# Layer 0 of a four-layer graph network: products of the matrices in two runs of four instead of in turn

## The chip, the cores and the metric

The kernel runs on one core of a Trainium2 chip as one program. The metric is the device time of one execution in microseconds. The engines are named as in the profile: PE is TensorE (PEld its weight loads), DVE is VectorE, ACT is ScalarE, POOL is GpSimd, and SP is SyncE, which here only issues DMAs.

## The reference

A graph has 8192 nodes with 32 features and 262144 edges, sorted by destination. Four layers follow each other, each of the form x = layernorm(x + layer(x)).

```
edge_index = jnp.stack([src, dst])
x = _layernorm(x + _L0_gnn_ref(x, L0_gnn_weight, src, dst, edge_type_64), axis=-1)   # sum over edges of x[src] @ weight[type]
x = _layernorm(x + _L1_gnn_ref(x, edge_index, edge_weight), axis=-1)                 # sum over edges of x[src] * edge_weight
x = _layernorm(x + _L2_gnn_ref(x, edge_index), axis=-1)                              # sum over edges of x[src]
x = _layernorm(x + _L3_gnn_ref(...), axis=-1)                                        # MLP on edge features, then messages and sums
```

In layer 0 each edge takes its source's features times one of 64 matrices of 32 x 32, and the results are summed by destination. Layers 1 and 2 sum plain features of the sources, with and without a weight per edge. In these two an edge's contribution depends only on (source, destination, weight), which do not change between layers.

## The kernel before

**Layer 0 itself.** A table `ytab` of x times every one of the 64 matrices is written to DRAM first. The edges are then taken in 256 groups of 8 tiles of 128 edges (`GG` = 256, `GT` = 8). For each group g, GpSimd gathers the rows of the table by 8 indirect DMAs (`gathers`, recorded at L454). VectorE builds one-hot matrices of the destinations (`pairs`, L583) and splits the gathered rows into three bfloat16 parts (`parts`, L858 to L863). TensorE multiplies the two, 8 matmuls (L897), which sums the rows by destination. VectorE collects a bank of sums every four groups (`bank_out`, L869). As soon as 1024 nodes have all their sums, `windows` (L575) puts them in place and `normalize` (L525 and the lines after it) adds and normalizes; the result goes to `x_b`.

**The matrices.** While layer 0 waits for its gathers, the same loop also builds two dense matrices for layers 1 and 2: for each destination node the weights and the counts of its edges by source, as a matrix of 128 x 64 each (source = low 7 bits by high 6 bits). `matrices(i)` does this for 32 destination nodes, 256 times in all, between groups 8 and 207. Each destination node has 64 slots for edges, and two nodes share the 128 partitions: the lower 64 hold one node's slots, the upper 64 the other's. VectorE makes one-hot matrices for 16 pairs of nodes: `oh_k` for the high bits (L638), `oh_l` for the low bits (L640), and `oh_k` times the weights (L643). There are two buffers of each (index b = i % 2), and VectorE waits for `oh_used[b]` before it writes one again.

TensorE then goes through four units (q = 0 to 3) of 8 products each (L654). A product has 64 slots as contraction, `oh_l` of one node (64 x 128) as weights and `oh_k` of the node (64 x 128: 64 columns of counts, 64 of weights) moving, all float32. It goes to one bank of PSUM: `two[:, h]` for h = 0 the lower node, h = 1 the upper node; j is the place of the product in the bank. A unit therefore fills two banks, and two units alternate (`pair_free[u]`). ScalarE evicts a unit by two instructions, the counts (L658) to 8 bits and the weights (L659) to float32. SyncE stores both to DRAM (`amat`, L664, 1 MB, and `cmat`, L666, 256 KB) once the four units are done.

**Layer 1 inside the loop.** Where a part of the matrices and of `x_b` is ready, layer 1 begins early: `layer1(g)` multiplies 1 MB pieces of `amat` that SyncE loads again (L695) with `x_b` (`products`, L717), 16 passes each. ScalarE takes a finished sum (L726), and in the next group TensorE turns it back (`turn_back`, L736) and VectorE adds it (`add_up`, L752). The list of which piece comes in which group is computed when the program is built (`plan`).

**The order of the work.** Every engine has one queue, in the order in which the program was written. For a group g that is:

```
pairs(oh[:, h], P, rel_b[:, g * GT:(g + 1) * GT])
PE.after(parts(g))
...                          # 8 matmuls at L897, marked as sums_of[g]
turn_back()
fetch_rows(g + AHEAD, 0, sums_of[g])
...                          # matrices(made): one or two for each group from 8 to 207
add_up()
fetch_rows(g + AHEAD, 1, now(PE))
layer1(g)
```

`AHEAD` is 12 here: GpSimd's first four gathers of group g + 12 wait for the sums of group g, and the last four for TensorE's last mark, which is the end of the matrices of group g. `Flow.after` is a wait on a semaphore, `Flow.mark` lets an instruction raise one.

After group 255, layers 1 and 2 are completed from the stored matrices, and layer 3 gathers, multiplies and sums again by edges. None of that is in the change.

Of the kernel before, what the change touches and what calls it, by code (L numbers as in the profile page):

```python
# [203 lines left out]
def raw_layers(tc, x, a, w0, w1, b1, w2, si, m, bad):  # L204
# [35 lines left out]
    def now(f):  # L240
        return (f.sem, f.n)

    def own(f, ins):

        mk = f.mark(ins)
        f.after(mk)
        return mk
# [383 lines left out]
    def matrices(i):  # L631

        b, pp, k0 = i % 2, i // 2, 16 * (i % 2)
        if i % WB == 0:
            V.after(now(V))
            own(V, V.e.tensor_copy(w_ps, meta_w.rearrange("p n k -> p (n k)")[:, i * 16:(i + WB) * 16]))
        V.after(oh_used[b])
        own(V, V.e.tensor_tensor(oh_k[:, b, :, 0, :], iota2[:, None, 0:64, 0].to_broadcast([P, 16, 64]),  # L638
                                 meta_k[:, pp, k0:k0 + 16, None].to_broadcast([P, 16, 64]), op=OP.is_equal))
        V.e.tensor_tensor(oh_l[:, b], iota2[:, None, :, 0].to_broadcast([P, 16, P]),  # L640
                          meta_l[:, pp, k0:k0 + 16, None].to_broadcast([P, 16, P]), op=OP.is_equal)
        wo = (i % WB) * 16
        vm = V.mark(V.e.tensor_tensor(oh_k[:, b, :, 1, :], oh_k[:, b, :, 0, :],  # L643
                                      w_ps[:, wo:wo + 16, None].to_broadcast([P, 16, 64]), op=OP.mult))
        PE.after(vm)
        for q in range(4):
            u = units[0] % 2
            units[0] += 1
            PE.after(pair_free[u])
            two = bank[:, 2 + 2 * u:4 + 2 * u, :]  # L650
            for j in range(4):
                for h in range(2):
                    hs_ = slice(64 * h, 64 * h + 64)
                    ins = PE.e.matmul(two[:, h].rearrange("p (c s j) -> p c s j", s=64, j=4)[:, :, :, j],  # L654
                                      oh_l[hs_, b, 4 * q + j, :], oh_k[hs_, b, 4 * q + j], start=True, stop=True)
            pm = PE.mark(ins)
            A.after(pm, st_ld[b].mark() if q == 0 and st_ld[b].n else None)
            A.e.activation(st_c[:, b, q], two[:, :, 0:256], AF.Copy)  # L658
            pair_free[u] = am = A.mark(A.e.activation(  # L659
                st_a[:, b, :, q].rearrange("p z h w -> p h z w"),  # L660
                two[:, :, 256:512].rearrange("p h (z w) -> p h z w", w=32), AF.Copy))
        oh_used[b] = pm
        S.after(am)
        st_ld[b].add(S.e.dma_start(amat[i // 128][i // 8 % 16, :, 0:P * 2048].rearrange("z (p w) -> p z w", w=2048)[:, :, 256 * (i % 8):256 * (i % 8 + 1)],  # L664
                                   st_a[:, b].rearrange("p z q h w -> p z (q h w)")))
        stored[i] = st_ld[b].add(S.e.dma_start(cmat[i], st_c[:, b].rearrange("p u h c -> p (u h c)")))  # L666
# [211 lines left out]
    for g in range(GG + 2):  # L878
# [9 lines left out]
        h, bk, c = g % NO, (g // per) % 2, g % per  # L888
# [13 lines left out]
        if g >= FIRST:  # L902
            upto = min(CB, (g - FIRST + 1) * CB // SP1)
            while made < upto:
                matrices(made)
                made += 1
# [835 lines left out]
```

## Time and profile before

| what | value |
|---|---|
| median of 10 runs | 5775.37 us (5768.69 to 5782.47) |
| profiled execution | 5773.13 us |
| its span, from first to last instruction | 5771.3 us |
| busy in the span: PE, DVE, POOL, ACT | 82%, 76%, 72%, 33% |
| weight loads (PEld) | 58% |
| mean granted TensorE clock | 0.893 |
| first and last instruction at L654 | about 362 and 2398 us |
| last gather of layer 0 issued, last normalization begun (L575) | 2805 us, 2811 us |

The page gives for each engine the time in which it did work. It also cuts the span into 40 slices of 144 us, with the busy share of each in tenths, and lists groups of instructions by line with their busy time, the mean duration of one, and the idle time of the engine before them with what ended it. [...] Row counts of matmuls and loads are passes: a float32 product takes two.

### The profile page before, as it was taken

To read this page: it belongs to the slowest core of one execution; us is meant where nothing else is said; L and a number is where in the kernel's file an instruction comes from. 1 tells how busy PE (TensorE), PEld (TensorE's weight loads), DVE (VectorE), ACT (ScalarE), POOL (GpSimd) and SP (SyncE) were. 2 spreads that over 40 slices of the span, in tenths; PEclk is the share of its full clock that TensorE was granted. 3 is DMA by queue.
4 is the path that set the end of the run, shared out by engine and by line. 5 is a ranking of instruction groups with operands and counts; after the bars stand their busy time and mean duration, and the time that the engine had idled before them with its cause. 6 is when DMAs were issued, how large, how long until landed. Compare 5 with 4: busy or idle time off the path is not lost.

```text
span 5771.3 us, 89081 instructions
## 1 busy us (share of the span) xinstructions
PE 4713.7 (82%) x34726; PEld 3355.1 (58%) x34726; DVE 4398.8 (76%) x9510; ACT 1894.0 (33%) x3067; POOL 4141.5 (72%) x4236
## 2 busy tenths in 40 slices
PE   7456677767777788644499999999999999999998
PEld 3146666666666666423255566666666666666665
DVE  4268898989989898543355788788787878888887
ACT  5255555555555555310176111111111111111110
POOL 2677777777777777777366777777777777777775
PEclk8578888989899899766699899999999999999999
DMA  9636666769789899955475111111111111111111
GB/s 344 223 100 201 190 211 223 253 229 330 243 299 315 281 339 324 350 176 203 187 279 197 26 26 30 30 26 30 26 30 30 26 30 26 30 26 30 30 26 22
DMA packets 583102, 865.29 MB, mean 150 GB/s; under 512 B 102605, under 2 KB 441614, under 8 KB 549134
## 3 DMA queue, kind: packets, MB, share of 16 engines
q1 hardware_dynamic: 448094, 782.68, 38.4%
q0 software_dynamic: 134144, 73.67, 6.6%
q8 instruction: 275, 4.51, 0.3%
q10 hardware_dynamic: 432, 3.15, 0.2%
q14 instruction: 157, 1.29, 0.1%
HBM read 454.28 MB, written 404.88 MB: 149 GB/s over the span
## 4 chain that ended last, share of the span: by engine, by line
PE 27%; POOL 10%; DMA 6%; DVE 4%; issue 4%; ACT 0%; POOLq 0%; DVEq 0%; ACTq 0%
PE bank L1203 11%; POOL f_arena L454 10%; PE bank L1194 9%; DMA f_arena<-fxtab,f_src 5%; PE bank L1033 4%; PE bank L1170 2%; DVE f_arena L1238 1%; PE bank L575 1%; DMA f_arena<-famat 1%; DVE f_arena L1234 1%; DVE f_arena L588 0%; PE bank L717 0%; PE bank L980 0%; DVE f_arena L1136 0%; DVE f_arena L1231 0%
## 5 line engine op out<-in xcount | busy, mean ns | idle before, releaser
L454 POOL DMA_INDIRECT f_arena<-fytab,f_row x2048 | 1957.2, 956 | 652.2 <-issue 548.6
L454 POOL DMA_INDIRECT f_arena<-fxtab,f_src x2048 | 1947.3, 951 | 643.1 <-issue 518.6
L654 PE MATMUL bank<-f_arena 64*128 64x128 f32 x16384 | 1195.8, 303 | 404.8 <-DVE f_arena L643 277.7
L654 PEld LDWEIGHTS bank<-f_arena 64*128 64x128 f32 x16384 | 1100.0, 210 | 484.8 <-DVE f_arena L643 302.6
L1203 PE MATMUL bank<-f_arena 128*128 128x344 f32 x4096 | 1311.2, 463 | 0.0
L1194 PE MATMUL bank<-f_arena 65*128 65x256 f32 x4096 | 1022.1, 393 | 79.0 <-DVE f_arena L1238 79.0
L1178 ACT ACTIVATE f_arena<-bank,f_arena 64x512 f32<-64x512 f32 x512 | 350.7, 685 | 2121.4 <-PE bank L1170 2114.8
L1194 PEld LDWEIGHTS bank<-f_arena 65*128 65x128 f32 x4096 | 771.1, 193 | 432.2 <-DVE f_arena L1238 145.7
L1203 PEld LDWEIGHTS bank<-f_arena 128*128 128x128 f32 x4096 | 799.2, 195 | 357.5 <-issue 29.8
L658 ACT ACTIVATE f_arena<-bank 128x512 uint8<-128x512 f32 x1024 | 613.1, 599 | 839.7 <-PE bank L654 742.5
L659 ACT ACTIVATE f_arena<-bank 128x512 f32<-128x512 f32 x1024 | 612.1, 598 | 0.0
L640 DVE TENSOR_TENSOR f_arena<-bank,f_arena 128x2048 f32<-128x2048 bf16 x256 | 586.6, 2292 | 8.7
L1238 DVE TENSOR_TENSOR f_arena<-bank,f_arena 128x256 f32<-128x256 f32 x1536 | 550.4, 413 | 0.0
L897 PE MATMUL bank<-f_arena 128*128 128x96 bf16 x2048 | 150.7, 225 | 313.0 <-DVE f_arena L863 312.9
L1134 DVE TENSOR_TENSOR f_arena<-f_arena 128x192 f32<-128x192 f32 x256 | 92.0, 359 | 408.0 <-DMA f_arena<-fxtab,f_src 406.4
L717 PE MATMUL bank<-f_arena,f_x_b 128*32 128x256 f32 x4096 | 307.9, 440 | 89.3 <-DMA f_arena<-famat 71.4
L588 DVE TENSOR_TENSOR f_arena<-bank,f_rel 128x512 f32<-128x512 f32 x512 | 348.7, 681 | 0.0
L1234 DVE TENSOR_TENSOR f_arena<-bank,f_arena 128x512 f32<-128x512 f32 x512 | 348.4, 680 | 0.0
L897 PEld LDWEIGHTS bank<-f_arena 128*128 128x128 bf16 x2048 | 109.6, 107 | 395.8 <-DVE f_arena L863 308.4
L638 DVE TENSOR_TENSOR f_arena<-bank,f_arena 128x1024 f32<-128x1024 bf16 x256 | 311.9, 1219 | 14.1 <-PE bank L654 12.0
L643 DVE TENSOR_TENSOR f_arena<-f_arena,bank 128x1024 f32<-128x1024 f32 x256 | 309.6, 1209 | 0.0
L802 POOL CAST f_arena<-f_arena 128x1536 bf16<-128x1536 uint8 x62 | 169.0, 2737 | 160.0 <-PE bank L717 70.3
(147 smaller groups left out, 4389.9 us busy)
## 6 DMA issues: line engine op xcount, KB each, us to landing
famat<-f_arena SPq DMA_DIRECT2D x256, 1024.0 KB
f_arena<-famat SPq DMA_DIRECT2D x256, 1024.0 KB, 12.0
fytab<-f_arena SPq DMA_DIRECT2D x64, 1024.0 KB, 11.9
fcmat<-f_arena SPq DMA_DIRECT2D x256, 256.0 KB
f_arena<-fcmat SPq DMA_DIRECT2D x16, 4096.0 KB, 14.4
f_arena<-fytab,f_row POOLq DMA_INDIRECT x2048
f_arena<-fxtab,f_src POOLq DMA_INDIRECT x2048
f_arena<-laid_ea SPq DMA_DIRECT2D x64, 512.0 KB, 3.4
```

Of the source, the lines that this page charges most:

```text
L454: return G.e.indirect_dma_start(out=dest, out_offset=None, in_=table, in_offset=bass.IndirectOffsetOnAxis(ap=ix, axis=0))
L588: return V.e.tensor_tensor(o, iota[:, None, :].to_broadcast([P, n, P]), rel[:, t:t + n, None].to_broadcast([P, n, P]), op=OP.is_equal)
L638: own(V, V.e.tensor_tensor(oh_k[:, b, :, 0, :], iota2[:, None, 0:64, 0].to_broadcast([P, 16, 64]), meta_k[:, pp, k0:k0 + 16, None].to_broa ...
L640: V.e.tensor_tensor(oh_l[:, b], iota2[:, None, :, 0].to_broadcast([P, 16, P]), meta_l[:, pp, k0:k0 + 16, None].to_broadcast([P, 16, P]), o ...
L654: ins = PE.e.matmul(two[:, h].rearrange("p (c s j) -> p c s j", s=64, j=4)[:, :, :, j], oh_l[hs_, b, 4 * q + j, :], oh_k[hs_, b, 4 * q + j ...
L658: A.e.activation(st_c[:, b, q], two[:, :, 0:256], AF.Copy)
L659: pair_free[u] = am = A.mark(A.e.activation(st_a[:, b, :, q].rearrange("p z h w -> p h z w"), two[:, :, 256:512].rearrange("p h (z w) -> p ...
L1178: quad[q + h] = dict(h=A.mark(A.e.activation(hs[0:64, (q + h) % 4], bank[64 * h:64 * h + 64, 2, :], AF.Relu, bias=b1_s[64 * h:64 * h + 64])))
L1194: ins = PE.e.matmul(wp[:, t, :], hs[0:65, q % 4, t * P:(t + 1) * P], w2_s[0:65], start=True, stop=True)
L1203: ins = PE.e.matmul(bank[:, g % 2, 0:MW], oh[:, c % NO, t, :], p[:, c % NP, t, :], start=(c % 2 == 0 and t == 0), stop=(c % 2 == 1 and t = ...
L1234: V.e.tensor_tensor(pq[:, :, 0:128].rearrange("p t (o k) -> p t o k", k=16), wp[:, :, 0:128].rearrange("p t (o k) -> p t o k", k=16), a0[: ...
L1238: ins = V.e.tensor_tensor(pq[:, :, 128 + 64 * mm:192 + 64 * mm].rearrange("p t (o i) -> p t o i", i=8), wp[:, :, 192:256].rearrange("p t ( ...
```

## The change

In each unit the two loops are exchanged. Before, the products go lower, upper, lower, upper (the j-th product of both nodes side by side). After, four products on the lower 64 partitions come first, then four on the upper 64. The operands, the places of the results, the number of instructions on every engine, and all waits and marks are the same; the unit's mark stands on the last product, which is the same product in both (j = 3, h = 1).

```diff
             two = bank[:, 2 + 2 * u:4 + 2 * u, :]
-            for j in range(4):
-                for h in range(2):
+            for h in range(2):
+                for j in range(4):
                     hs_ = slice(64 * h, 64 * h + 64)
                     ins = PE.e.matmul(two[:, h].rearrange("p (c s j) -> p c s j", s=64, j=4)[:, :, :, j],
                                       oh_l[hs_, b, 4 * q + j, :], oh_k[hs_, b, 4 * q + j], start=True, stop=True)
             pm = PE.mark(ins)
```

## The prediction

> **What bounds the kernel now.** I read the page's slices first, one slice being 144 us.
>
> ```profile
> PE   7456677767777788644499999999999999999998
> DVE  4268898989989898543355788788787878888887
> POOL 2677777777777777777366777777777777777775
> PEclk8578888989899899766699899999999999999999
> ```
>
> The change lives in layer 0, slices 3 to 19. TensorE is at 6 to 8 there, VectorE at 8 and 9, and GpSimd's 7 never moves. The groups of instructions explain GpSimd's flat 7, and show the matmuls of L654, the line that is reordered.
>
> ```profile
> L454 POOL DMA_INDIRECT f_arena<-fytab,f_row x2048 | 1957.2, 956 | 652.2 <-issue 548.6
> L654 PE MATMUL bank<-f_arena 64*128 64x128 f32 x16384 | 1195.8, 303 | 404.8 <-DVE f_arena L643 277.7
> ```
>
> A gather takes 0.944 us (median) and then 0.30 us before the next one is issued ("issue": it waits for nothing). In windows, the stretch that holds all of L654:
>
> ```profile
> core 0: us, PE busy (x) PEld busy (x) DVE busy (x) ACT busy (x) POOL busy (x), PEclk, DMA share, GB/s
> 360.00:2400.00 2040.00, 1536.13 (x21208) 1328.83 (x21208) 1823.25 (x2428) 1111.71 (x2167) 1542.03 (x1635) 0.90 0.79 265
> ```
>
> 1635 gathers in 2040 us are one per 1.248 us: GpSimd is never free. A group of edges needs 8 gathers, so the pace is 9.98 us a group. The chain of waits says the same at the end of layer 0: gather, issue, gather, issue, up to the last gather at 2805 us, and then 6 us to the first matmul of the last normalization. So GpSimd bounds layer 0. VectorE (1823 of 2040 us) is close behind; TensorE has 504 us idle: 278 us waiting for VectorE's L643, 121 for ScalarE's L659, and at other lines 51 for L863, 34 for loads of the matrices and 13 for L726.
>
> How far is GpSimd ahead of the rest when the matrices end? The groups of instructions from 0 to 2400.2 us:
>
> ```profile
> L454 POOL DMA_INDIRECT f_arena<-fytab,f_row x1723 | 1650.5, 958 | 553.1 <-issue 460.8 <-DMA fytab<-f_arena 28.4 <-PE bank L654 21.6
> L897 PE MATMUL bank<-f_arena 128*128 128x96 bf16 x1664 | 113.6, 215 | 121.6 <-DVE f_arena L863 121.5
> ```
>
> 1723 gathers are 215.4 groups, 1664 matmuls at L897 are 208 groups: GpSimd leads by 7.4 groups. The code lets it lead by 12, because the gathers of group g+12 wait for the sums of group g. So the other engines may fall behind by 4.6 groups more, 46 us, before GpSimd has to stop. After that, lost time is lost for good: 36 groups of gathers, 359 us, are then still to be issued.
>
> **What the change costs on TensorE.** Per unit nothing is added or removed: 8 products of 2 passes each, so 16 weight loads and 16 matmuls, the two evictions and the semaphores are the same. Only the order differs. The timeline of two units that wait for nothing between them:
>
> ```profile
> 1199.72 2.06 PE L654 MATMUL bank<-f_arena 64*128 64x128 f32 x32 [1.22 <-DVE f_arena L643]
> 1199.72 1.86 PEld L654 LDWEIGHTS bank<-f_arena 64*128 64x128 f32 x32 [1.36 <-DVE f_arena L643]
> ```
>
> The last matmul's 0.27 us off, 1.79 us remain for 32 passes: 0.056 us a pass, though a pass takes 0.27 us. Passes come as pairs, one on the lower 64 rows and one on the upper: in narrower windows the two loads of a pair start 7 ns apart, and pairs follow each other every 0.111 us. So two halves work at once, 8 pairs make a unit, 8 x 0.111 = 0.89 us.
>
> What does one set of rows do alone? The timeline shows it where consecutive passes all use the same rows, with the same 128 columns moving, and with 32:
>
> ```profile
> 958.76 1.05 PE L575 MATMUL bank<-f_arena,f_shift 128*128 128x128 f32 x7
> 1211.94 0.52 PEld L736 LDWEIGHTS bank<-f_stack,f_arena 128*128 128x128 f32 x4 [0.23 <-ACT f_arena L726]
> ```
>
> L736: (0.52 - 0.19 for the last) / 3 = 0.110 us from load to load, with hardly anything moving, so it is the load of 128 float32 columns that takes 0.11 us. L575: 1.05 less 0.275 for the last matmul and 0.107 for the first load is 0.67 us for six steps, 0.111 us each: the 128 columns move while the next weights load. So one set of rows makes a pass every 0.111 us, exactly what each half does today. After the change the second half stands idle while the first makes 8 passes. Only at a seam do both work: the first load of the other half needs no room that is in use and can go beside the last load of this half, as loads pass a waiting matmul at the start of each unit now. A unit is then 14 steps from start to start, 1.56 us. ScalarE adds a little: a unit's bank is free 1.49 us after its last matmul starts (0.32 until L658 starts, 1.08 for both evictions, the rest signals); two units later that makes 15 x 0.111 + 1.49 = 3.16 us where TensorE needs 3.12, so I take 1.58 us a unit. I bound it by 14 steps (1.55) below and 16 (1.78, nothing beside anything) above, and stay near the lower end, since its mechanism is visible in the trace.
>
> [...]
>
> **TensorE's whole path from 360 us to the sums of group 208.** In issue time, counts from the same stretch:
> - L654: 1024 units x 1.58 + 256 last steps x 0.11 = 1646 us (now 0.89 x 1024 = 911 at best, near 1240 with waits between units and the slow clock).
> - L717: 2688 passes = 168 products, each 16 passes; the timeline has 32 in 1.93 us, so 0.96 each: 161 us.
> - L736: 424 x 0.111 = 47 us. L897: 199 groups x 0.39 (8 in 0.51 us, less most of the last one's 0.2) = 78 us. L575: 120 passes, about 0.16 each: 19 us.
>
> Sum 1951 us. Waits come on top. L863, the loads and L726 do not depend on the order: 51 + 34 + 13 = 98. The six normalizations in the stretch hold VectorE, and thereby TensorE, for 54 us (L525 on L575) plus 27 (on ScalarE): 82. These 180 are the lower end. Most of L643's 278 us goes, since TensorE now comes late to what VectorE has ready: VectorE needs about 4.6 us per step of matrices (L638, L640, L643) and 3.1 per group, TensorE 6.4 per step. But VectorE's L752 waits for TensorE's turn-back products (64 us now), and they stand in the queue behind the longer units of the group before; VectorE then starts the next step of matrices later. Half of L643 kept gives the upper end, 320. I take 230, nearer the lower end.
>
> Clock: 0.90 granted over the stretch, 0.95 in its busiest 200 us (1960 to 2160, TensorE busy 83%). With the gaps gone I take 0.97: 6% of 2200 us at half speed costs 65, of which I count half, 35 us, the rest falling in waits.
>
> End: 360 + 1951 + 230 + 35 = 2576 us instead of 2400, 176 us later. GpSimd's free lead takes 46, which leaves **+130 us**. What follows has cover: 48 groups without matrices need about 4 us of VectorE each, GpSimd gives them only every 9.98 us, and today the first 24 of them pass in 180 us. Evictions, stores and loads are the same in number, DMA (0.79 busy here) has more time for them. Layers 1 to 3 after 2811 us are untouched. The profiled execution took 5773.1 us (span 5771.3, and 1.8 around it), 2.2 under the median of 5775.4; 5775 + 130 = **5905 us**.
>
> **Rivals.** (a) No overlap at the seams, 16 steps a unit: 0.20 us x 1024 = 205 us more work, of which some 75 disappears in waits that no longer occur: +260, 6035 us. For it: the order of issue is strictly as written in the rows of before; against it: loads already pass waiting matmuls. Chance 0.17.
> (b) Not slower: GpSimd's lead hides it. It decides at 46 us: TensorE must reach group 208 by 2446 us. That leaves 2446 - 360 - 1951 = 135 us for all waits and the slow clock, under the 180 that do not depend on the order. It gives 5775 us, or a little less if stores and loads collide less. Chance 0.05.
> (c) The change does not do what it says: the queue reaches past four products and starts the upper rows early, a unit stays at 0.89 us, 5775 us. In the rows of before, matmuls start in the order of the program without exception that I found. Chance 0.04.
> (d) A load is not hidden under a matmul of its own rows after all, a step of 0.11 for the load plus 0.05 to 0.11 for the stream, 2.2 to 3.1 us a unit: over 600 us slower. Chance 0.03.
> My forecast has the remaining 0.71.
>
> **How the numbers follow.** Within the forecast, waits of 180 without a cold clock give +45, waits of 320 with twice the cold share +255. Rival (a) at +260 lies at the upper end, with the cold clock's second share at +290. I take 5825 to 6060 (+50 to +285); (b), (c), (d) and the tails stay out. About 0.2%, 12 us, is what a measurement of this kernel can tell from no change. Slower by more: 0.71 + 0.17 + 0.03 = 0.91; within: most of (b) and (c), 0.07; faster, when less pressure on the DMA queues helps and nothing costs: 0.02.
>
> **What would show it.** Right: two units at L654 take 3.1 to 3.4 us in the timeline instead of 2.06, the loads of a unit 0.11 us apart with no second one beside them except at seams; busy time at L654 rises to about 1700 us, the idle time on L643 falls below 150, on L659 below 40; GpSimd gets waits for TensorE of 100 us or more before 2600 us; the clock in the stretch is above 0.95; the last gather is 130 us later, and what comes after takes as long as before. Wrong: pairs still 0.111 us apart with both halves in them (c), gathers without a gap (b), a step of 0.2 us (d), a unit of 1.78 us (a), or time that changes behind the last gather.

## The result, and the profile after

The changed kernel takes 5831.6 us (median of 9 runs, 5819.8 to 5845.7), the kernel before 5775.4. The ratio is 1.010, with a 95% interval from 1.0091 to 1.0109: 56 us slower, where +130 was forecast. The profiled execution took 5819.6 us (span 5817.8), 12 us below its median, and is compared below with that of before, whose span of 5771.3 us is 46.5 us shorter.

From the page after, two rows of the slices and two groups of instructions:

```profile
PE   7468888889889899855389899999999999999998
PEclk7578999989899899866699899999999999999999
L454 POOL DMA_INDIRECT f_arena<-fytab,f_row x2048 | 1957.6, 956 | 699.6 <-issue 545.6
L654 PE MATMUL bank<-f_arena 64*128 64x128 f32 x16384 | 1533.0, 299 | 179.4 <-DVE f_arena L643 117.0
```

L654 is busy for 1533 us instead of 1196, with the same number of passes, and its idle time falls from 405 to 179 us. The gathers of layer 0 (first L454 row) take the same time, but GpSimd's idle time before them grows from 652.2 to 699.6 us: 47.4 us, the whole difference of the two executions. The last gather is issued at 2851.4 us instead of 2805.3, and what comes behind it takes as long as before.

The windows view over the stretch of the matrices (columns as in the prediction's fence):

```profile
355.00:2478.00 2123.00, 1867.73 (x21216) 1670.72 (x21216) 1826.67 (x2430) 1153.75 (x2167) 1577.47 (x1672) 0.93 0.76 255
```

TensorE is now busy for 1868 of 2123 us and idle for 255, half of before. The granted clock is 0.93, not the 0.97 that I took.

The groups of instructions from 0 to 2478.1 us, when the sums of group 208 begin (2400.3 in the kernel before):

```profile
L454 POOL DMA_INDIRECT f_arena<-fytab,f_row x1758 | 1684.0, 958 | 599.7 <-issue 468.8 <-PE bank L654 46.4 <-DMA fytab<-f_arena 27.9
L897 PE MATMUL bank<-f_arena 128*128 128x96 bf16 x1664 | 113.9, 215 | 112.2 <-DVE f_arena L863 112.2
```

1758 gathers are 219.75 groups, 11.75 ahead of the 208 that are summed: the lead is used up to its limit of 12. The waits in 355 to 2478 us (who waits for whom, total us, times, longest):

```profile
PE bank L654 <- DVE f_arena L643: 117.0, 84, 4.1
DVE f_arena L752 <- PE bank L736: 114.7, 41, 12.7
PE bank L654 <- ACT f_arena L659: 47.3, 52, 7.1
POOL f_arena L454 <- PE bank L654: 46.4, 78, 7.9
POOL f_arena L454 <- PE bank L897: 12.8, 14, 4.9
```

The same in the kernel before, 360 to 2400 us:

```profile
PE bank L654 <- DVE f_arena L643: 277.7, 134, 4.5
PE bank L654 <- ACT f_arena L659: 121.0, 244, 7.1
POOL f_arena L454 <- PE bank L654: 21.6, 71, 0.3
```

There GpSimd waited for L654 in 71 places and at most 0.3 us, which is its usual time between gathers. Now single waits last up to 7.9 us. The timeline of GpSimd shows one:

```profile
2427.81 0.94 POOL L454 DMA_INDIRECT f_arena<-fytab,f_row  x1 [0.30 <-issue]
2434.93 0.94 POOL L454 DMA_INDIRECT f_arena<-fytab,f_row  x1 [6.17 <-PE bank L654]
2436.17 0.94 POOL L454 DMA_INDIRECT f_arena<-fytab,f_row  x1 [0.30 <-issue]
```

So the way from TensorE to the kernel's time is the predicted one: TensorE's longer path first eats GpSimd's lead, then stops the gathers. The size is off by more than half. The records of L654 show where: the last product of a unit raises a semaphore, so the units can be told apart. Medians over the 256 steps of matrices, in us:

| from | before | after | forecast |
|---|---|---|---|
| first load to the last matmul of unit 1 | 0.89 | 1.44 | 1.66 |
| last matmul of unit 1 to that of unit 2 | 0.89 | 1.11 | 1.56 to 1.58 |
| unit 2 to unit 3 (waits for ScalarE) | 1.45 | 1.78 | 1.58 |
| unit 3 to unit 4 | 0.98 | 1.11 | 1.58 |
| a step of matrices, median | 4.24 | 5.43 | 6.43 |
| a step of matrices, mean | 4.85 | 5.94 | |

A unit that follows another takes 10 steps of 0.111 us, not 14.

### The profile page after: what moved, and what is told of

It reads as the page before. It is cut to its first block, busy times and chain, and to the rows that moved or that the text cites. A ratio compares the mean times of both kernels' runs of the same rounds, so it can differ in the third digit from the quotient of the medians.

```text
span 5817.8 us, 89081 instructions
## 1 busy us (share of the span) xinstructions
PE 5041.5 (87%) x34726; PEld 3695.9 (64%) x34726; DVE 4400.5 (76%) x9510; ACT 1935.9 (33%) x3067; POOL 4142.5 (71%) x4236
## 4 chain that ended last, share of the span: by engine, by line
PE 26%; POOL 11%; DMA 6%; issue 4%; DVE 4%; ACT 0%; POOLq 0%; DVEq 0%; ACTq 0%
POOL f_arena L454 11%; PE bank L1203 11%; PE bank L1194 8%; DMA f_arena<-fxtab,f_src 5%; PE bank L1033 4%; PE bank L1170 2%; DVE f_arena L1238 1%; DMA f_arena<-famat 1%; PE bank L575 1%; DVE f_arena L588 0%; DVE f_arena L1234 0%; PE bank L980 0%; PE bank L717 0%; DVE f_arena L1136 0%; DVE f_arena L1134 0%
## 5 line engine op out<-in xcount | busy, mean ns | idle before, releaser
L454 POOL DMA_INDIRECT f_arena<-fytab,f_row x2048 | 1957.6, 956 | 699.6 <-issue 545.6
L454 POOL DMA_INDIRECT f_arena<-fxtab,f_src x2048 | 1947.8, 951 | 643.5 <-issue 518.7
L654 PE MATMUL bank<-f_arena 64*128 64x128 f32 x16384 | 1533.0, 299 | 179.4 <-DVE f_arena L643 117.0
L654 PEld LDWEIGHTS bank<-f_arena 64*128 64x128 f32 x16384 | 1442.7, 200 | 250.6 <-DVE f_arena L643 129.8
L659 ACT ACTIVATE f_arena<-bank 128x512 f32<-128x512 f32 x1024 | 606.6, 592 | 0.0
L897 PE MATMUL bank<-f_arena 128*128 128x96 bf16 x2048 | 150.8, 225 | 273.6 <-DVE f_arena L863 273.6
L897 PEld LDWEIGHTS bank<-f_arena 128*128 128x128 bf16 x2048 | 109.7, 107 | 356.0 <-DVE f_arena L863 268.5
L643 DVE TENSOR_TENSOR f_arena<-f_arena,bank 128x1024 f32<-128x1024 f32 x256 | 309.6, 1209 | 0.0
```

The lines of the kernel that those rows point to most:

```text
L454: return G.e.indirect_dma_start(out=dest, out_offset=None, in_=table, in_offset=bass.IndirectOffsetOnAxis(ap=ix, axis=0))
L659: pair_free[u] = am = A.mark(A.e.activation(st_a[:, b, :, q].rearrange("p z h w -> p h z w"), two[:, :, 256:512].rearrange("p h (z w) -> p ...
```

## The experiments

A pass is one weight load and one matmul, a step is the 0.111 us from one pass on a half to the next, and a seam is a place where the order goes from one half to the other.

**Theory A**: TensorE looks several passes ahead in its queue and starts the other rows' loads and matmuls before this half's run is done; what is left of the loss is covered by GpSimd's lead as far as it goes. Against it: **B**, as in the prediction, one load beside another at each seam; **C**, the slower clock and not the order; **D**, GpSimd's lead plays no part; **E**, the evictions behind the later last product are a good part of the loss; **F**, a short lead costs by itself.

The experiments ran in five sessions. In three of them the kernel before itself took 7349 to 7411 us: TensorE paused before passes of the matrices for up to 7 us with no wait that the profile shows ("issue": 236 times before the loads of one line in runs_of_two, 558.8 us in all, the longest 7.1), at a granted clock near 0.80. Times from there are only compared within their session.

**The probe.** Ahead of the groups, products of the same form on constant data, in runs of r:

```diff
     PE.after(*freed)
+    probe = lambda h, j: (bank[:, 2 + h, 128 * (j % 4):128 * (j % 4) + 128], ident[64 * h:64 * h + 64, :], ident[64 * h:64 * h + 64, :])
+    ...                                          # 48 products in turn, ahead of the timed ones
+    for k in range(24 // (2 * r)):               # written out for r = 1, 2, 3, 4, 6, 12
+        for j in range(r):
+            ins = PE.e.matmul(*probe(0, r * k + j), start=True, stop=True)
+        for j in range(r):
+            ins = PE.e.matmul(*probe(1, r * k + j), start=True, stop=True)
+    own(PE, ins)                                 # wait for its own end
+    ...                                          # 24 products on the lower rows alone
```

> The changed kernel with a probe ahead of the groups: after 48 products to warm the clock, TensorE runs 24 products of the same form as the change's (64 rows, 128 float32 columns, 2 passes each) in runs of 1, 2, 3, 4, 6 and 12 on the lower rows and then as many on the upper, and at last 24 on the lower rows alone; between the parts it waits for its own end, and nothing else uses the results. Theory A (TensorE looks ahead past 3 or 4 waiting passes and starts the other rows early; a step is 0.111 us): 24, 24 to 25, 26 to 27, 28 to 33, 36 to 39 and 44 to 45 steps, that is 2.7, 2.7 to 2.8, 2.9 to 3.0, 3.1 to 3.7, 4.0 to 4.3 and 4.9 to 5.0 us from first load to last matmul, and 48 steps, 5.3 us, for the lower rows alone. Theory B (as in the prediction, one load beside the last load at each seam): 24, 37, 41, 43, 45, 47 and 48 steps, so 4.1 us already for runs of two and 4.8 for runs of four.

From first load to last matmul, the records give 2.68 us for runs of one product, 2.78 for two, 3.00 for three and 3.66 for four: 24, 25, 27 and 33 steps of 0.111 us. The parts with runs of twelve and with the lower rows alone ran at 0.213 us a step: 9.50 and 10.19 us, 44.6 and 47.8 steps. In the kernel before, steps at L654 took 0.213 us (median) where the trace has the granted clock at 0.5, and 0.112 where it has it at 1.0, so I put these two parts down to half the clock and the others to the full one. The part with runs of six fell into pauses and says nothing. B would have had 37, 41 and 43 steps for two, three and four: it is wrong. A depth of 3, fitted to these times, gives every one of them: a pass started when the oldest one not yet started was at most three passes before it (worked out so, runs of twelve take 45 steps). The timeline of the loads at the seam of the runs of twelve shows it directly (L868 is the lower half, L870 the upper):

```profile
285.84 0.76 PEld L868 LDWEIGHTS bank<-f_ident 64*128 64x128 f32 x3
286.48 0.28 PEld L870 LDWEIGHTS bank<-f_ident 64*128 64x128 f32 x1
286.48 0.33 PEld L868 LDWEIGHTS bank<-f_ident 64*128 64x128 f32 x1
286.65 0.33 PEld L870 LDWEIGHTS bank<-f_ident 64*128 64x128 f32 x1
286.69 0.33 PEld L868 LDWEIGHTS bank<-f_ident 64*128 64x128 f32 x1
286.86 0.33 PEld L870 LDWEIGHTS bank<-f_ident 64*128 64x128 f32 x1
286.91 0.33 PEld L868 LDWEIGHTS bank<-f_ident 64*128 64x128 f32 x1
287.07 4.60 PEld L870 LDWEIGHTS bank<-f_ident 64*128 64x128 f32 x21
```

The upper half's first load starts while three loads of the lower half are still to come, and three upper ones run beside them. The last part, on the lower rows alone, shows each load issued 0.005 us after the matmul before it on the same rows, and a pass every 0.213 us, while a matmul lasts 0.417 (median): here loads lay beside matmuls of their own rows.

**The changed kernel on two lines.** The same instructions, the two loops written apart:

```diff
-            for h in range(2):
-                for j in range(4):
-                    ...
+            for j in range(4):
+                ins = PE.e.matmul(...)           # lower rows, L652 in the profile
+            for j in range(4):
+                ins = PE.e.matmul(...)           # upper rows, L655
```

> The changed kernel itself, its two loops written on two lines, beside the kernel before on the same chip. All theories: 56 us over the kernel before if this chip runs without the pauses of the one used first. Theory A also says what the two lines show: in a unit without a wait, the first load of the upper rows starts together with the sixth of eight loads of the lower rows, a unit follows the other after 10 steps of 0.111 us (1.11 us), a unit after a wait takes 13 (1.44 us).

5830.4 us against 5774.5, ratio 1.0089 (1.0072 to 1.0106). The timeline of the loads in a unit after a wait:

```profile
1252.54 0.74 PEld L652 LDWEIGHTS bank<-f_arena 64*128 64x128 f32 x6 [0.26 <-ACT f_arena L660]
1253.10 0.29 PEld L655 LDWEIGHTS bank<-f_arena 64*128 64x128 f32 x2
1253.20 0.19 PEld L652 LDWEIGHTS bank<-f_arena 64*128 64x128 f32 x1
1253.31 0.19 PEld L655 LDWEIGHTS bank<-f_arena 64*128 64x128 f32 x1
1253.32 0.19 PEld L652 LDWEIGHTS bank<-f_arena 64*128 64x128 f32 x1
```

Six lower loads from 1252.54 (the sixth at about 1253.09), and the first upper one at 1253.10: beside the sixth of eight, as A said. And the matmuls of the same seam:

```profile
1253.20 0.27 PE L652 MATMUL bank<-f_arena 64*128 64x128 f32 x1
1253.31 0.27 PE L655 MATMUL bank<-f_arena 64*128 64x128 f32 x1
1253.32 0.27 PE L652 MATMUL bank<-f_arena 64*128 64x128 f32 x1
1253.42 0.27 PE L655 MATMUL bank<-f_arena 64*128 64x128 f32 x1
1253.43 0.27 PE L652 MATMUL bank<-f_arena 64*128 64x128 f32 x1
```

The upper half's matmul at 1253.31 starts ahead of two lower ones that stand before it in the program. In these rows matmuls start in the order of the program within a half, but not across the halves.

**Runs of two.**

```diff
-            for h in range(2):
-                for j in range(4):
+            for j0 in (0, 2):
+                for h in range(2):               # written out
+                    for j in (j0, j0 + 1):
```

> Half of the change: two products on the lower rows, two on the upper, and again. Theory A (look-ahead of 3 to 4 passes): a run of 4 passes is within reach, a unit takes 9 to 10 steps, 1.0 to 1.1 us, and the time is within 10 us of the kernel before. Theory B (one load beside another at each seam): 12 to 13 steps, 1.35 us, as long as the changed kernel's unit takes now, and so about as slow as that kernel, 50 us over before. Theory C (it isn't the order but the slower clock that costs): no statement on the steps, the time follows the granted clock.

> Runs of two products again, on a chip that may run without pauses. Theory A (the queue reaches 3 passes past the oldest waiting one, as the probe showed): a unit after a wait takes 9 steps (1.00 us, in the kernel before 0.89), the others 8, so a step of matrices 4.3 us instead of 4.2: within 12 us of the kernel before. Theory B' (every run on the same rows costs, by its number of seams): more than half of the changed kernel's loss, 30 us or more.

In a session without pauses: 5774.2 us against 5774.5, ratio 0.9997 (0.9987 to 1.0006). A unit after a wait takes 0.99 us and the next 0.89, a step of matrices 4.41 (median), as A says; group 208 comes at 2407.8 us, 7.5 later, and GpSimd's lead hides that. In the session with pauses: 7427.0 against 7401.1, 1.0033 (1.0023 to 1.0043), 26 us. Where GpSimd is not the bound, that small loss is not covered; I expected less than 10. Runs on one half did not cost as such: with runs of 4 passes, a unit that follows another took the same 0.89 us as in the kernel before. B' (every run costs by its seams) is out. So is C as the first cause: the changed kernel's granted clock is the higher one, 0.93 against 0.90 while the matrices are made. And it was 0.889 in the profiled execution here and 0.887 in split_evict below, under the 0.893 of the kernel before, and neither loses time.

**The lead at 8, 12 and 14 groups.** The kernels before and after with

```diff
-    AHEAD = 12
+    AHEAD = 8                                    # or 14
```

> The changed kernel (its two loops written on two lines of their own), with AHEAD at 8 instead of 12 in layer 0: GpSimd may lead by 8 groups only. Theory A: the lead of GpSimd pays for part of the loss. In the kernel before it is 7.4 groups at group 208, so almost nothing is left to give, and the change costs its whole 78 us (group 208 later by that) plus some 10 behind it: 80 to 95 us over the kernel before. Theory D (the lead has no part in it, the time is what TensorE's path loses): the same 56 us as with 12. The two lines show which half a pass belongs to: A expects matmuls of the upper rows to start before the last ones of the lower rows.

> The kernel before with AHEAD at 8. Its lead never needs more than 7.4 groups, so theory A expects no more than 5 us over the kernel before. If the shorter lead costs by itself, through gathers that come late for a group, it would be more than that, and after_ahead8 is then to be compared with this run.

> The changed kernel with GpSimd's lead in layer 0 limited to 8 groups. Theory A: 80 to 95 us over the kernel before, because the 44 us that the lead of 12 gives are no longer there. Theory D (the lead has no part): 56 us.

> The kernel before with GpSimd's lead in layer 0 limited to 8 groups. Theory A: its lead reaches 7.4 groups without the limit, so the limit costs at most 5 us, and the 100 us of after_ahead8_b over the kernel before are the change's loss without the cover. Rival F: a short lead costs by itself (gathers that come too late in other places), 20 us or more.

> The changed kernel with the lead in layer 0 widened from 12 to 14 groups. Theory A: two more groups of gathers, 2 x 9.98 us, are issued before the matrices end, so it is 20 us faster than the changed kernel, some 36 us over the kernel before. Theory D (the lead has no part) and F: no difference from the changed kernel, 56 us.

> The kernel before with the lead limited to 8 groups, once more on a chip that may run without pauses. Theory A: at most 5 us over the kernel before, since its lead reaches 7.4 groups without a limit. Rival F (a short lead costs by itself): 20 us or more.

> The changed kernel with a lead of up to 14 groups, once more on a chip that may run without pauses. Theory A: 20 us faster than the changed kernel, some 36 us over the kernel before. Theories D and F: no difference from the changed kernel, 51 to 56 us over the kernel before.

> The changed kernel, for comparison on the same chip as the next two. Without pauses: 51 to 56 us over the kernel before. On a chip where TensorE pauses (the kernel before takes about 7400 us there and GpSimd waits for TensorE already): nothing covers TensorE's longer steps, so 1.09 us x 256 or more come through, 150 to 280 us.

> The changed kernel with a lead of up to 14 groups. Theory A without pauses: 20 us faster than the changed kernel. With pauses: no gain over the changed kernel, since TensorE sets the pace from the first group on and a longer lead is used up at once. Theories D and F without pauses: no difference.

> The kernel before with a lead of 8 groups. Theory A without pauses: at most 5 us over the kernel before; F: 20 us or more. With pauses: 25 to 35 us faster than the kernel before, as three runs on such a chip showed.

Without pauses, GpSimd's idle time at the gathers of layer 0 is that of the profiled execution, and the difference in time is that of the medians to the kernel before in the same session:

| kernel | lead allowed | GpSimd idle at L454, us | over the kernel before, us | ratio |
|---|---|---|---|---|
| before | 12 | 652.2 | | |
| before_ahead8_d | 8 | 662.1 | 15 | 1.0030 (1.0018 to 1.0041) |
| after_ahead8_b | 8 | 745.2 | 100 | 1.0175 (1.0157 to 1.0192) |
| after | 12 | 699.6 | 56 | 1.0100 (1.0091 to 1.0109) |
| after_two_lines_d | 12 | 711.5 | 54 | 1.0092 (1.0076 to 1.0109) |
| after_ahead14_d | 14 | 677.5 | 31 | 1.0056 (1.0039 to 1.0073) |

Each group of lead is worth about 11 us, close to the 9.98 of one group of gathers: from 8 to 12 groups the changed kernel gains 44 us, from 12 to 14 another 23. D is out. The kernel before at 8 costs 15 us, more than the 5 that I expected. Without the limit its lead peaks at 8.9 groups (at group 210), not at the 7.4 of group 208; with the limit it stands at 8.0 there. That accounts for the 10 us by which GpSimd's idle time grows, not for the other 5. After_ahead8_b's 100 lie 5 over the expectation of 80 to 95; less the 15 that the limit costs by itself they are 85. F's threshold of 20 is not reached.

With pauses, all is different: GpSimd's idle time at L454 is near 1800 us already in before_ahead8, 793 of it waiting for L654, and its lead of 8 is used up, 7.4 groups or more from group 12 to 199. There after_ahead8 was 1.0187 of the kernel before (1.0172 to 1.0202; 145 us), after_ahead14 1.0276 (1.0257 to 1.0295; 200 us), after_ahead14_c 1.0237 (1.0220 to 1.0254; 176 us), and before_ahead8, _b and _c 0.9953, 0.9966 and 0.9956 (intervals within 0.9940 to 0.9979; 26 to 36 us less). For the kernel before, less lead does not hurt there. The changed kernel with its own lead of 12 was not run with pauses, so what the lead is worth to it there stays open. That a shorter lead is even faster there was not looked into, nor what the pauses are.

**Evictions by half.**

```diff
-            PE.after(pair_free[u])
+            PE.after(half_free[u][0])            # then the lower products
             ...
-            A.after(pm, ...)                     # both evictions, after all eight products
+            A.after(pm, ...)                     # evict counts and weights of the lower half
+            PE.after(half_free[u][1])            # then the upper products, and their two evictions
```

> The changed order, but each half of a unit gets its own mark, its own two evictions (256 columns instead of 2 x 256) and its own wait, so that ScalarE empties the lower half's bank while the upper half is computed. Theory E (a third of a longer step of matrices is TensorE waiting for ScalarE, 1.78 us where 1.11 would do, since the evictions begin only after the last product of both halves): that wait goes, a step of matrices takes 4.8 us instead of 5.4, and the time is within 15 us of the kernel before. Against it (the new order alone costs, the evictions are hidden): no gain, 50 us or more over the kernel before, and more if twice as many evictions fill ScalarE.

5777.2 us against 5774.5, ratio 1.0005 (0.9995 to 1.0014): no loss that could be measured. A step of matrices takes 4.76 us (median) instead of 5.43, every half 0.554 us after the last. From the waits of this kernel in 360 to 2430 us (L652 is the lower half, L657 its last eviction):

```profile
PE bank L652 <- DVE f_arena L643: 188.6, 101, 4.5
PE bank L652 <- ACT f_arena L657: 39.7, 21, 6.1
```

The wait for ScalarE is down to 21 places from 52, and the longer wait for VectorE (117.0 us in the changed kernel) shows that TensorE comes early again. Group 208 comes at 2423.8 us, still 23.5 later than before; the lead goes to 11.5 groups, and the gathers have no gap (GpSimd idle 652.1 us). The time is as expected, but it doesn't show E. The kernel before waits for ScalarE as well: in its median step, units 3 and 4 take 1.45 and 0.98 us where 0.89 would do, 0.65 us together, against 0.67 in the changed kernel, and TensorE's idle time on L659 is 121.0 us before and 47.3 after. The 1.19 us by which the median step grew are the longer units: 0.55 for the first and some 0.22 for each of the others make 1.2. Evictions by half take away a wait that both orders have, 0.67 us of the 1.19; GpSimd's lead covers what is left. The old order with evictions by half was not run.

No version here beats the kernel before: without pauses GpSimd's gathers set the end of layer 0, and nothing in these edits makes them shorter.

## Why the prediction was right and wrong

**Right: what bounds it, the direction, and the way the loss goes.** GpSimd without a gap before, gaps of up to 7.9 us on L654 after, an end moved by what the lead did not cover, and nothing behind the last gather: all as put down. The +56 us lie at the low end of the range from +50 to +285, and that is luck, as the sum below shows. Of the signs, the idle time on L643 came out (117 us, under 150); L654's busy time (1533 us, not 1700), the idle time on L659 (47, not under 40), the clock (0.93, not above 0.95) and GpSimd's waits for TensorE (46 us on L654 and 13 on L897, not 100) did not.

**Wrong: the step "only at a seam do both work", as one load beside another.** The term of L654 was 1646 us, from 14 steps a unit, and 14 was also its lower bound. The depth of three passes that was fitted to the probe gives 10 steps for a unit following another (1.11 us measured) and 13 for one after a wait (1.44 us measured). With the wait for ScalarE (1.78 us once in a step of matrices) that makes 5.43 us for each of the 256 instead of 6.43: 256 us less. The argument from the rows of before was that matmuls start in the order of the program, "without exception that I found". There, lower and upper passes alternate, and one following the other tells nothing of what TensorE would do with a longer run. Rival (c), that the queue reaches past the run, is what the starts showed in part, at a chance of 0.04 and with the wrong end: upper passes started up to three passes early, not eight.

**Wrong: the clock.** The term was 35 us, for a clock of 0.97. The clock was 0.93. 202 of the 256 steps of matrices took 5.43 us, the other 54 took 7.84 on average, which is 130 us more. The granted clock was at half for a part of 44 of the 54, and these hold 123 of the 130 us; a pass took 0.213 us there instead of 0.111. The kernel before has such steps too: its mean is 0.61 us over its median, 156 us in all, and 138 of them lie in 72 steps at half the clock. So the slow clock is a term that the prediction had too small, but no more of it came with the change.

**Roughly right: the other work and the waits.** Between the last matmul of one step and the first load of the next lie 2.33 us on average, 595 us in all. Less the 305 us of other products this leaves 290 of waits, where 230 were taken, inside the 180 to 320.

**The sum.** 360 + 256 x 5.94 + 595 = 2476 us, against 2478 measured for group 208 and 2576 forecast: 78 us late, not 176. The 256 us of the first error were partly given back by the clock (95) and the waits (60). With 1390 us for L654 and all other terms as the prediction had them, group 208 would have come at 360 + 1695 + 230 + 35 = 2320 us, before the 2400 of the kernel before, and the forecast would have been no loss at all. The range holds the measured time because errors of opposite sign met. (By its own terms, rival (a)'s 260 with the clock's second 35 is 295, not 290; nothing rests on it.)

**Wrong: the lead.** 46 us were read off at group 208. The lead of the kernel before still grows to 8.9 groups at 210, so only 3.1 groups, 31 us, were free. 78 - 31 = 47, which is GpSimd's added idle time. Had the lead been the 46 us of the prediction, the loss would have been 32.

## What to carry to other kernels

Here the order of the passes left both halves of the array filled as long as the runs on one half were short: runs of 4 passes cost next to nothing (4.41 us a step of matrices instead of 4.24), while with runs of 8 a unit of 8 steps took 10 (1.11 us), and 13 after a wait (1.44 us). An engine off the path may lose what the bound engine's lead can cover (31 of the 78 us here), and the lead is to be read at its peak (8.9 groups), not where the loss is booked (7.4). Where an engine waits for a buffer that another one empties, give each part its own mark as soon as it is complete: the evictions by half took TensorE's wait out of the median step, and with them the new order cost nothing that could be measured. A fix that wins the loss back does not show that it removes the loss's cause; look whether the kernel before has the same wait.

## What the runs showed of the hardware that was not expected

Matmuls on the upper 64 rows started ahead of up to three passes on the lower rows that stand before them in the program, and across a unit's end lower ones ahead of up to three upper ones (after_two_lines). A reach of 3 passes (each a load and a matmul) fits every part of the probe with runs of two products or more that ran without pauses (25, 27, 33 and 44.6 steps for runs of two, three, four and twelve). A pass on one half, 128 float32 columns loaded and 128 moved, took 0.11 us where the trace has the granted clock at 1.0 and 0.213 where it has it at 0.5, whether or not the other half worked beside it: 0.112 and 0.213 with both at work (L654 in the kernel before), 0.110 and 0.213 with one alone (the first five loads of a unit after a wait, in the changed kernel; medians).

The same kernel took 5770 to 5790 us in some sessions and 7350 to 7410 in others, with TensorE halting for up to 7 us before a unit of the matrices (7.1 in runs_of_two, 6.7 in before_ahead8) and about 1 us inside one (0.76 at 1507.20 us of before_ahead8) while no wait is shown. The record names the same chip, number 3, for a session with pauses (before_ahead8_c) and one without (before_ahead8_d).
